# All products but the scores in two halves of 64 columns; the experts' rows turned by VectorE, fetched by blocks of channels

## The chip, the core and the metric

The kernel runs on one core of a Trainium2 chip. A core has TensorE (PE; its weight loads are listed apart as PEld), VectorE (DVE), ScalarE (ACT), GpSimd (POOL) and SyncE (SP, which only issues transfers). TensorE multiplies from SBUF into PSUM, which has eight banks here. Transfers between SBUF and the chip's memory run on 16 DMA engines, and are issued by SP, ACT or GpSimd in the order of each queue. The metric is the device time of one execution, in microseconds; the median of the runs shown is compared.

## The reference

One transformer block on x of 8 x 512 tokens and 256 channels, all in f32. After a layernorm, attention (with a low-rank key/value path) and a mixture of experts run beside each other on the same xn, and both are added to x:

```
xn = layernorm(x)
latent = xn @ w_kv_down                       # 256 -> 128
k, v = split(latent @ w_kv_up)                # 16 heads of 64 each
q = xn @ w_q
att = softmax(causal(q k^T / 8));  y = att v
attention = y @ w_out
scores = sigmoid(xn @ gate_w.T + lb_bias);  top 2 of 8 experts per token
for e in range(8):
    y_e = (silu(xn @ eg[e].T) * (xn @ eu[e].T)) @ ed[e].T     # inner width 128
    moe += where(e chosen, y_e * wmean[e], 0)
shared = (silu(xn @ sg.T) * (xn @ su.T)) @ sd.T               # inner width 256
out = x + attention + moe + shared
```

## The kernel before, in words

The work is cut into 64 pairs of heads: 8 batches of 512 tokens times 8 pairs of the 16 heads. A loop over the pairs writes each engine's order by hand; a plan (`put`, `put_half`) says at which place within a pair's step (0 to 2) the other work is dropped in. Engines follow these orders strictly. TensorE, VectorE, ScalarE, SP and later GpSimd are all ordered in this way.

For each pair, `keys`, `queries` and `values` (L569, L578, L559) are products of weights with the transposed activations; `scores` (L606) multiplies q and k of two heads with a contraction of 64, the two heads in the two row halves of the array. VectorE adds the mask and takes a minimum (L613), ScalarE takes the exponential (L620), VectorE turns the result in 32x32 blocks (`transposed`, L633, L640), and sixteen transfers move the blocks to where they are needed (`moved`, pt<-blk, L652, on SP and GpSimd). Two pairs later `weighted` (L695) multiplies with v: its output has 64 rows for each of two heads, so the two heads use the two column halves of the array. `inverse_sums` (L669 to L674) and `spread_sums` (rb<-row, L682) bring the softmax's sums; GpSimd scales (L708). `project` (L720) multiplies by w_out and takes the shared expert's second product into the same bank; `shared_hidden` (L461) is its first part. All of the products other than scores and `weighted` are full 128x128 ones.

In the first part of the loop the layernorm of the coming batches runs beside the attention: statistics on VectorE, `normalise` (L269) on GpSimd (VectorE for the first batch), `turn` (L279) transposes on TensorE, `logits` (L288). Each token's normalised row goes with its own number in column 256 (a row has 272 columns in all) into `xns`. Then a router on VectorE sorts tokens by expert, and GpSimd scatters the rows into `xg_d` in memory (L440), in 39 tiles of 256 slots, each tile of one expert.

From pair 18 on, the 39 expert tiles run beside the attention. `expert_fetch` gathers the tile's weights (L476, GpSimd) and loads its 256 rows in one transfer on SP (xg<-xg_d, L483). `expert_turn` transposes them on TensorE (four transposes into ps_x, L491), ScalarE copies the result to SBUF (xgT, L493), and GpSimd copies the token numbers (to, L495). `expert_hidden` (ps_e, L503) and `expert_down` (ps_ed, L516) are the products, `expert_add` (L527) adds the result's rows to the output in memory by the token numbers. `expert_fetch` is planned four half steps before the tile's half h, `expert_turn` at the start of step h // 2.

At the start SP and ACT load x and the weights (L135 to L161); a contraction over 256 channels is cut into two chunks of 128, chunk c with the channels 128c to 128c + 127 in the partitions.

Of the kernel before, what the change touches and what calls it, by code (L numbers as in the profile page):

```python
# [29 lines left out]
F32 = mybir.dt.float32  # L33
I32 = mybir.dt.int32
# [14 lines left out]
def kernel(  # L49
# [59 lines left out]
    def bank(shape, name):  # L109

        return psum.tile(shape, F32, tag="w", name=name)

    xf = x.rearrange("b t c -> (b t) c")
    outf = out.rearrange("b t c -> (b t) c")

# [15 lines left out]
    def load_x(b, first=0, count=NQ, by=nc.sync):  # L131
        if b not in xins:
            xins[b] = lnp.tile([P, NQ, C], F32, bufs=3, name="xin")
        n = b * NQ + first
        by.dma_start(  # L135
            xins[b][:, ds(first, count), :],
            xf[ds(n * P, count * P), :].rearrange("(n p) c -> p n c", p=P),
        )

    load_x(0, 0, NQ // 2)  # L140
    load_x(0, NQ // 2, NQ // 2, nc.scalar)
    gate_sb = const.tile([P, NCC, E], F32, name="gate_sb")
# [7 lines left out]
    wq_sb = wts.tile([P, NCC, HD], F32, name="wq_sb")  # L150
    nc.sync.dma_start(wq_sb, w_q.rearrange("(c p) m -> p c m", p=P))
# [3 lines left out]
    nc.sync.dma_start(sg_sb, sg_w)  # L155
    su_sb = wts.tile([P, NCC, NS * P], F32, name="su_sb")
    nc.sync.dma_start(su_sb, su_w)
# [298 lines left out]
    def shared_hidden(b, u):  # L456
        pss = []
        for w in (sg_sb, su_sb):
            ps = bank([P, T], "ps_gu")
            for cc in range(NCC):  # L460
                nc.tensor.matmul(  # L461
                    ps, w[:, cc, ts(u, P)], xnTs[b][:, cc, :],
                    start=(cc == 0), stop=(cc == NCC - 1),
                )
            pss.append(ps)
        th = hp.tile([P, T], F32, name="th")
        h = hp.tile([P, T], F32, tag=f"h{u}", name="h")
        swiglu(*pss, th, h)
        shared[b, u] = h

    fetched, turned, hidden = {}, {}, {}

    def expert_fetch(t):

        w = ep.tile([P, WR], F32, bufs=4, name="w")
        nc.gpsimd.indirect_dma_start(  # L476
            out=w[:, :],
            out_offset=None,
            in_=wall_d[:, :],
            in_offset=bass.IndirectOffsetOnAxis(ap=wrow_i[:, t : t + 1], axis=0),  # L480
        )
        xg = ep.tile([P, NU, W], F32, bufs=3, name="xg")
        nc.sync.dma_start(xg, xg_d[ts(t, SLOTS), :].rearrange("(u p) c -> p u c", p=P))  # L483
        fetched[t] = w, xg

    def expert_turn(t):
        xg = fetched[t][1]
        ps = bank([P, NCC, SLOTS], "ps_x")
        for u in range(NU):
            for cc in range(NCC):  # L490
                nc.tensor.transpose(ps[:, cc, ts(u, P)], xg[:, u, ts(cc, P)], ident)  # L491
        xgT = ep.tile([P, NCC, SLOTS], F32, bufs=2, name="xgT")
        nc.scalar.copy(xgT, ps)  # L493
        to = ep.tile([P, NU], I32, bufs=4, name="to")
        nc.gpsimd.tensor_copy(to, xg[:, :, C].bitcast(I32))  # L495
        turned[t] = xgT, to

    def expert_hidden(t):
        w = fetched[t][0]
        ps = bank([P, 2, SLOTS], "ps_e")  # L500
        for v, at in enumerate((WG, WU)):
            for cc in range(NCC):
                nc.tensor.matmul(  # L503
                    ps[:, v, :], w[:, ds(at + cc * I, I)], turned[t][0][:, cc, :],
                    start=(cc == 0), stop=(cc == NCC - 1),
                )
        th = ep.tile([P, SLOTS], F32, name="the")
        h = ep.tile([P, SLOTS], F32, name="he")
        swiglu(ps[:, 0, :], ps[:, 1, :], th, h)
        hidden[t] = h  # L510

    def expert_down(t):
        w = fetched[t][0]
        ps = bank([P, NU, C], "ps_ed")
        for u in range(NU):
            nc.tensor.matmul(  # L516
                ps[:, u, :], hidden[t][:, ts(u, P)], w[:, ds(WD, C)], start=True, stop=True
            )
# [6 lines left out]
    def expert_add(t, u):  # L525

        nc.gpsimd.indirect_dma_start(  # L527
            out=acc_d[:, :],
            out_offset=bass.IndirectOffsetOnAxis(ap=turned[t][1][:, u : u + 1], axis=0),
            in_=results[t][:, u, :],  # L530
            in_offset=None,
            compute_op=ALU.add,
        )
# [9 lines left out]
    def latent(b):  # L543
        ps = bank([P, T], "ps_lat")
        for cc in range(NCC):
            nc.tensor.matmul(  # L546
                ps, wkd_sb[:, cc, :], xnTs[b][:, cc, :],
                start=(cc == 0), stop=(cc == NCC - 1),
            )
        lats[b] = qkp.tile([P, T], F32, name="lat")  # L550
        nc.scalar.copy(lats[b], ps)  # L551

    def values(b, g, half):

        if half == 0:
            vs[b, g] = vp.tile([P, NQ, VH * D], F32, name="v")
        ps = bank([P, 2, VH * D], "ps_v")
        for u in range(2):
            nc.tensor.matmul(  # L559
                ps[:, u, :],  # L560
                lats[b][:, ts(2 * half + u, P)],
                wkv_sb[:, ds(HD + g * VH * D, VH * D)],
                start=True, stop=True,
            )
        nc.scalar.copy(vs[b, g][:, ts(half, 2), :], ps)

    def keys(b, p):
        ps = bank([P, T], "ps_k")
        nc.tensor.matmul(ps, wkv_sb[:, ts(p, P)], lats[b], start=True, stop=True)  # L569
        ks[b, p] = qkp.tile([P, T], F32, name="k")  # L570
        nc.scalar.copy(ks[b, p], ps)

    def queries(b, p):


        ps = bank([P, T], "ps_q")
        for cc in range(NCC):
            nc.tensor.matmul(  # L578
                ps, wq_sb[:, cc, ts(p, P)], xnTs[b][:, cc, :],
                start=(cc == 0), stop=(cc == NCC - 1),  # L580
            )
        qs[b, p] = qkp.tile([P, T], F32, name="q")
        nc.scalar.mul(qs[b, p], ps, QSCALE)
# [127 lines left out]
    def project(b, tt, ps=None, first=0, last=NS + NPAIR):  # L711


        n = b * NQ + tt
        if ps is None:
            ps = bank([P, C], "ps_o")
        ops = [(yTs.get((b, p)), wo_sb[:, p, :]) for p in range(NPAIR)]
        ops[NPAIR - 2 : NPAIR - 2] = [(shared[b, u], sd_sb[:, u, :]) for u in range(NS)]
        for k, (l, r) in list(enumerate(ops))[first:last]:
            nc.tensor.matmul(  # L720
                ps, l[:, ts(tt, P)], r, start=(k == 0), stop=(k == len(ops) - 1)
            )
# [280 lines left out]
```

## Time and profile before

| | us |
|---|---|
| three runs: median | 955.46 |
| lowest, highest | 953.57, 957.12 |
| the profiled execution, its own time | 949.33 |
| its span on the core | 947.5 |
| granted TensorE clock, mean | 0.987 |

The page lists groups of instructions by line, engine and operation: how many, their busy time and the mean of one, then the idle time of the engine just before them and what ended it. A line "X <- Y" among the waits says that X waited until Y was done: total time, times, and the longest. The chain of work that ended last gives 76% to TensorE, 9% to transfers and 4% to VectorE:

```profile
PE 76%; DMA 9%; DVE 4%; POOL 3%; SPq 3%; issue 2%; ACT 1%; ACTq 0%; DVEq 0%; POOLq 0%
```

Busy time of TensorE counts modelled ends, which overlap the next start, so times of its groups are best read from the starts.

### The profile page before, as it was taken

To read this page: it belongs to the slowest core of one execution; us is meant where nothing else is said; L and a number is where in the kernel's file an instruction comes from. 1 tells how busy PE (TensorE), PEld (TensorE's weight loads), DVE (VectorE), ACT (ScalarE), POOL (GpSimd) and SP (SyncE) were. 2 spreads that over 40 slices of the span, in tenths; PEclk is the share of its full clock that TensorE was granted. 3 is DMA by queue.
4 is the path that set the end of the run, shared out by engine and by line. 5 is a ranking of instruction groups with operands and counts; after the bars stand their busy time and mean duration, and the time that the engine had idled before them with its cause. 6 is when DMAs were issued, how large, how long until landed. Compare 5 with 4: busy or idle time off the path is not lost.

```text
span 947.5 us, 16101 instructions
## 1 busy us (share of the span) xinstructions
PE 912.2 (96%) x4316; PEld 557.6 (59%) x4316; DVE 580.0 (61%) x2041; ACT 504.3 (53%) x1467; POOL 610.2 (64%) x846
## 2 busy tenths in 40 slices
PE   8899898989999979999999999999999999999998
PEld 4355456644455446766667656676666775656656
DVE  3877753897636756356774466743677446675571
ACT  3656553445535546446674366744567545665550
POOL 3698984537887954646766667664767646765560
PEclk9899999999999999999999999999999999999999
DMA  7589888776767789667887777876878868776793
GB/s 274 162 254 283 272 265 296 200 215 207 222 186 187 234 218 220 143 168 183 214 200 171 189 179 176 225 169 160 192 185 207 205 146 196 190 154 147 186 275 96
DMA packets 127449, 190.63 MB, mean 201 GB/s; under 512 B 24896, under 2 KB 88640, under 8 KB 127120
## 3 DMA queue, kind: packets, MB, share of 16 engines
q1 hardware_dynamic: 87728, 103.54, 39.3%
q0 software_dynamic: 37152, 82.52, 36.1%
q10 hardware_dynamic: 2480, 3.55, 1.4%
q8 instruction: 36, 0.59, 0.3%
q14 instruction: 53, 0.43, 0.2%
HBM read 66.45 MB, written 50.18 MB: 123 GB/s over the span
## 4 chain that ended last, share of the span: by engine, by line
PE 76%; DMA 9%; DVE 4%; POOL 3%; SPq 3%; issue 2%; ACT 1%; ACTq 0%; DVEq 0%; POOLq 0%
PE ps_o L720 13%; PE ps_y L695 13%; PE ps_s L606 12%; PE ps_q L578 9%; PE ps_e L503 7%; DMA pt<-blk 5%; PE ps_v L559 4%; PE ps_k L569 4%; PE ps_gu L461 4%; PE ps_ed L516 4%; SPq L652 3%; PE ps_x L491 2%; DMA rb<-row 2%; DVE blk L633 1%; PE ps_lat L546 1%
## 5 line engine op out<-in xcount | busy, mean ns | idle before, releaser
L613 DVE CUSTOM_DVE_ANT_0 ps_s<-ps_s,mask 128x128 f32<-128x128 f32 (+3 forms) x512 | 238.7, 519 | 177.8 <-PE ps_s L606 174.6
L620 ACT ACTIVATE pr<-ps_s,mn 128x128 f32<-128x128 f32 (+3 forms) x512 | 271.1, 538 | 143.6 <-DVE mn L613 113.8
L633 DVE STREAM_TRANSPOSE blk<-pr 128x384 f32<-128x384 f32 (+2 forms) x512 | 207.4, 446 | 26.3 <-ACT yT L707 6.9
L652 POOL DMA_DIRECT2D pt<-blk x303 | 161.5, 654 | 50.6 <-DVE ri L669 21.3
L527 POOL DMA_INDIRECT acc_d<-ye,to x78 | 127.4, 1634 | 91.3 <-issue 29.2
L606 PE MATMUL ps_s<-k,q 64*128 64x128 f32 (+3 forms) x1024 | 167.0, 448 | 6.7 <-ACT pr L620 6.0
L695 PE MATMUL ps_y<-pt,v 128*64 128x512 f32 (+3 forms) x1024 | 153.4, 442 | 10.0 <-DMA pt<-blk 6.3
L708 POOL TENSOR_TENSOR yT<-yT,rb 128x512 f32<-128x512 f32 x62 | 83.0, 1338 | 90.1 <-ACT yT L707 79.1
L606 PEld LDWEIGHTS ps_s<-k,q 64*128 64x128 f32 x1024 | 91.0, 186 | 79.0 <-issue 46.2
L578 PE MATMUL ps_q<-xnT,wq_sb 128*128 128x512 f32 x256 | 124.8, 611 | 0.0
L695 PEld LDWEIGHTS ps_y<-pt,v 128*64 128x64 f32 x1024 | 69.3, 137 | 91.9 <-issue 64.3
L720 PE MATMUL ps_o<-wo_sb,yT 128*128 128x256 f32 x512 | 120.5, 380 | 2.0 <-POOL yT L708 2.0
L620 ACT ACTIVATION_READ_ACCUMULATOR pr<-ps_s,mn 128x1 f32 x512 | 108.7, 212 | 0.0
L720 PEld LDWEIGHTS ps_o<-wo_sb,yT 128*128 128x128 f32 x512 | 96.7, 190 | 17.9 <-POOL yT L708 2.4
L578 PEld LDWEIGHTS ps_q<-xnT,wq_sb 128*128 128x128 f32 x256 | 50.6, 198 | 58.0 <-issue 52.5
L503 PE MATMUL ps_e<-xgT,w 128*128 128x256 f32 x312 | 75.0, 383 | 2.4 <-ACT xgT L493 2.4
L569 PE MATMUL ps_k<-lat,wkv_sb 128*128 128x512 f32 x128 | 71.4, 641 | 1.0 <-ACT lat L551 1.0
L613 DVE DVE_READ_ACCUMULATOR2_ANT mn<- 128x1 f32 x512 | 72.2, 141 | 0.0
L440 POOL DMA_INDIRECT xg_d<-xn,at_i x64 | 62.8, 981 | 14.3 <-issue 12.9
L503 PEld LDWEIGHTS ps_e<-xgT,w 128*128 128x128 f32 x312 | 58.3, 190 | 21.9 <-ACT xgT L493 13.7
L559 PE MATMUL ps_v<-wkv_sb,lat 128*128 128x256 f32 x256 | 67.4, 386 | 0.0
L559 PEld LDWEIGHTS ps_v<-wkv_sb,lat 128*128 128x128 f32 x256 | 46.8, 190 | 31.3 <-issue 18.6
(132 smaller groups left out, 974.9 us busy)
## 6 DMA issues: line engine op xcount, KB each, us to landing
pt<-blk SPq DMA_DIRECT2D x681, 80.0 KB
pt<-blk POOLq DMA_DIRECT2D x303, 80.0 KB
rb<-row SPq DMA_DIRECT2D x128, 128.0 KB
xg_d<-zero POOLq DMA_DIRECT2D x26, 408.0 KB
xg<-xg_d SPq DMA_DIRECT2D x39, 272.0 KB
acc_d<-in_x_dram POOLq DMA_DIRECT2D x8, 512.0 KB
xin<-in_x_dram SPq DMA_DIRECT2D x7, 512.0 KB
xnT_d<-lnT SPq DMA_DIRECT2D x7, 512.0 KB
```

Of the source, the lines that this page charges most:

```text
L503: nc.tensor.matmul(ps[:, v, :], w[:, ds(at + cc * I, I)], turned[t][0][:, cc, :], start=(cc == 0), stop=(cc == NCC - 1),)
L527: nc.gpsimd.indirect_dma_start(out=acc_d[:, :], out_offset=bass.IndirectOffsetOnAxis(ap=turned[t][1][:, u : u + 1], axis=0), in_=results[t ...
L559: nc.tensor.matmul(ps[:, u, :], lats[b][:, ts(2 * half + u, P)], wkv_sb[:, ds(HD + g * VH * D, VH * D)], start=True, stop=True,)
L569: nc.tensor.matmul(ps, wkv_sb[:, ts(p, P)], lats[b], start=True, stop=True)
L578: nc.tensor.matmul(ps, wq_sb[:, cc, ts(p, P)], xnTs[b][:, cc, :], start=(cc == 0), stop=(cc == NCC - 1),)
L606: nc.tensor.matmul(pss[j][:, ds(at, n)], q[ts(j, D), ts(i, P)], k[ts(j, D), :n], start=True, stop=True,)
L613: nc.vector.tensor_tensor_reduce(out=pss[j][:, ds(at, n)], in0=pss[j][:, ds(at, n)], in1=mask[:, T - n :], scale=1.0, scalar=NO_MIN, op0=A ...
L620: nc.scalar.activation(o, s, AF.Exp, bias=mn, scale=-1.0, accum_out=rs[:, j, i : i + 1])
L633: nc.vector.transpose(blk[:, :, j, i : i + (nr - 1) * (NQ - 1) + 1 : NQ - 1, :].rearrange("p b c q -> p c b q"), pr[:, j, : nr * P].rearra ...
L652: by.dma_start(pt[ts(kb, QB), a], blks[b, p][ts(a, QB), kb])
L695: nc.tensor.matmul(ps[ts(j, D), :, c:, :], vs[b, h // VH][:, c, ts(h % VH, D)], pts[b, p][:, :, j, at : at + NQ - c, :], start=(c == 0), s ...
L720: nc.tensor.matmul(ps, l[:, ts(tt, P)], r, start=(k == 0), stop=(k == len(ops) - 1))
```

## The change

1. A helper `product` replaces the full matmul in `latent`, `keys`, `queries`, `values`, `project`, `shared_hidden`, `expert_hidden` and `expert_down`: it makes each product as two matmuls with 64 columns of the weights each, into partitions 0 to 63 and 64 to 127 of the same bank, with the same moving operand. `scores`, `weighted`, `turn`, `logits` and the router's sums stay as they are.
2. `expert_turn` is one VectorE transpose in 32x32 blocks, from SBUF to SBUF, and stands near the end of the step before (place 0.8 of step h // 2 - 1) instead of at the start of step h // 2. TensorE's transposes, ScalarE's copy and GpSimd's copy of token numbers go.
3. For that, `expert_fetch` loads xg with 32 slots in the partitions, in four transfers on SP, one for each block of 64 columns of the row, in pieces of 64 elements. The token numbers of three tiles come in one transfer on ACT.
4. The channels of a row are stored in another order: `normalise` writes runs of 32 channels (`by_chunk`), and wkd, wq, gate, sg and su are loaded in four transfers each (`load_weights`), 32 partitions apiece, with their channels in that order. wq is loaded by ACT, right after its half of x; the gate's weights and bias come later, on SP. The experts' own weights and the remaining loads are unchanged.

```diff
+    def product(out, lhsT, rhs, start, stop):
+        for j in range(2):
+            nc.tensor.matmul(
+                out[ts(j, D)], lhsT[:, ts(j, D)], rhs, start=start, stop=stop
+            )
+    def by_chunk(a):
+        return a.rearrange("p (a c k) -> p c a k", a=NB, k=QB)
...
+    def load_weights(w_sb, w, by=nc.sync):
+        for a in range(NB // NCC):
+            for c in range(NCC):
+                by.dma_start(
+                    w_sb[ds((a * NCC + c) * QB, QB)],
+                    w.rearrange("(x a k) c m -> a c k x m", x=NCC, k=QB)[a, c],
+                )
...
-    gate_sb = const.tile([P, NCC, E], F32, name="gate_sb")
-    nc.scalar.dma_start(gate_sb, gate_w)
-    lb_sb = const.tile([P, E], F32, name="lb_sb")
-    nc.scalar.dma_start(lb_sb, lb_bias.broadcast_to([P, E]))
     wkd_sb = wts.tile([P, NCC, R], F32, name="wkd_sb")
-    nc.sync.dma_start(wkd_sb, w_kv_down.rearrange("(c p) r -> p c r", p=P))
+    load_weights(wkd_sb, w_kv_down.rearrange("(c p) r -> p c r", p=P))
+    wq_sb = wts.tile([P, NCC, HD], F32, name="wq_sb")
+    load_weights(wq_sb, w_q.rearrange("(c p) m -> p c m", p=P), nc.scalar)
...
             by.tensor_scalar(
-                xns[:, n, :C], xins[n // NQ][:, n % NQ, :], mv[:, n, 0:1], rstd[:, n : n + 1],
-                ALU.subtract, ALU.mult,
+                by_chunk(xns[:, n, :C]),
+                xins[n // NQ][:, n % NQ, :].rearrange("p (c a k) -> p c a k", a=NB, k=QB),
+                mv[:, n, 0:1], rstd[:, n : n + 1], ALU.subtract, ALU.mult,
             )
...
-        xg = ep.tile([P, NU, W], F32, bufs=3, name="xg")
-        nc.sync.dma_start(xg, xg_d[ts(t, SLOTS), :].rearrange("(u p) c -> p u c", p=P))
+        xg = ep.tile([P, SLOTS // QB, NCC * QB], F32, bufs=3, name="xg")
+        for a in range(NB):
+            nc.sync.dma_start(
+                xg[ts(a, QB)],
+                xg_d[ts(t, SLOTS), ts(a, NCC * QB)].rearrange("(t q) c -> q t c", q=QB),
+            )
+        if t % NZ == 0:
+            to = ep.tile([P, NZ * NU], I32, bufs=3, name="to")
+            nc.scalar.dma_start(
+                to,
+                xg_d[ts(t // NZ, NZ * SLOTS), C : C + 1]
+                .bitcast(I32).rearrange("(n p) c -> p (n c)", p=P),
+            )
...
     def expert_turn(t):
-        xg = fetched[t][1]
-        ps = bank([P, NCC, SLOTS], "ps_x")
-        for u in range(NU):
-            for cc in range(NCC):
-                nc.tensor.transpose(ps[:, cc, ts(u, P)], xg[:, u, ts(cc, P)], ident)
         xgT = ep.tile([P, NCC, SLOTS], F32, bufs=2, name="xgT")
-        nc.scalar.copy(xgT, ps)
-        to = ep.tile([P, NU], I32, bufs=4, name="to")
-        nc.gpsimd.tensor_copy(to, xg[:, :, C].bitcast(I32))
-        turned[t] = xgT, to
+        nc.vector.transpose(
+            xgT.rearrange("p c (t q) -> p t c q", q=QB),
+            fetched[t][1].rearrange("p t (c k) -> p t c k", k=QB),
+        )
+        turned[t] = xgT
...
-                nc.tensor.matmul(
-                    ps[:, v, :], w[:, ds(at + cc * I, I)], turned[t][0][:, cc, :],
+                product(
+                    ps[:, v, :], w[:, ds(at + cc * I, I)], turned[t][:, cc, :],
                     start=(cc == 0), stop=(cc == NCC - 1),
                 )
...
-        put(h // 2, 0.1, expert_turn, t)
+        put(h // 2 - 1, 0.8, expert_turn, t)
```

More of the change, by code (lines that the diff above doesn't have):

```diff
@@ L138, in load_x @@
         )
+    def load_weights(w_sb, w, by=nc.sync):
[5 more added lines that the diff above has]
+                )
     load_x(0, 0, NQ // 2)
     load_x(0, NQ // 2, NQ // 2, nc.scalar)
-    gate_sb = const.tile([P, NCC, E], F32, name="gate_sb")
-    nc.scalar.dma_start(gate_sb, gate_w)
-    lb_sb = const.tile([P, E], F32, name="lb_sb")
-    nc.scalar.dma_start(lb_sb, lb_bias.broadcast_to([P, E]))
     wkd_sb = wts.tile([P, NCC, R], F32, name="wkd_sb")
-    nc.sync.dma_start(wkd_sb, w_kv_down.rearrange("(c p) r -> p c r", p=P))
+    load_weights(wkd_sb, w_kv_down.rearrange("(c p) r -> p c r", p=P))
+    wq_sb = wts.tile([P, NCC, HD], F32, name="wq_sb")
+    load_weights(wq_sb, w_q.rearrange("(c p) m -> p c m", p=P), nc.scalar)
     wkv_sb = wts.tile([P, 2 * HD], F32, name="wkv_sb")
     nc.sync.dma_start(wkv_sb[:, :HD], w_kv_up[:, :HD])
-    wq_sb = wts.tile([P, NCC, HD], F32, name="wq_sb")
-    nc.sync.dma_start(wq_sb, w_q.rearrange("(c p) m -> p c m", p=P))
+    gate_sb = const.tile([P, NCC, E], F32, name="gate_sb")
+    load_weights(gate_sb, gate_w)
+    lb_sb = const.tile([P, E], F32, name="lb_sb")
+    nc.sync.dma_start(lb_sb, lb_bias.broadcast_to([P, E]))
     nc.sync.dma_start(wkv_sb[:, HD:], w_kv_up[:, HD:])
@@ L154 @@
     sg_sb = wts.tile([P, NCC, NS * P], F32, name="sg_sb")
-    nc.sync.dma_start(sg_sb, sg_w)
+    load_weights(sg_sb, sg_w)
     su_sb = wts.tile([P, NCC, NS * P], F32, name="su_sb")
-    nc.sync.dma_start(su_sb, su_w)
+    load_weights(su_sb, su_w)
     sd_sb = wts.tile([P, NS, C], F32, name="sd_sb")
@@ L469, in shared_hidden @@
         shared[b, u] = h
-    fetched, turned, hidden = {}, {}, {}
+    fetched, tokens, turned, hidden = {}, {}, {}, {}
     def expert_fetch(t):
@@ L481, in expert_fetch @@
         )
-        xg = ep.tile([P, NU, W], F32, bufs=3, name="xg")
-        nc.sync.dma_start(xg, xg_d[ts(t, SLOTS), :].rearrange("(u p) c -> p u c", p=P))
+        xg = ep.tile([P, SLOTS // QB, NCC * QB], F32, bufs=3, name="xg")
[11 more added lines that the diff above has]
+            )
+            for u in range(NZ):
+                tokens[t + u] = to[:, ts(u, NU)]
         fetched[t] = w, xg
     def expert_turn(t):
-        xg = fetched[t][1]
-        ps = bank([P, NCC, SLOTS], "ps_x")
-        for u in range(NU):
-            for cc in range(NCC):
-                nc.tensor.transpose(ps[:, cc, ts(u, P)], xg[:, u, ts(cc, P)], ident)
-        xgT = ep.tile([P, NCC, SLOTS], F32, bufs=2, name="xgT")
-        nc.scalar.copy(xgT, ps)
-        to = ep.tile([P, NU], I32, bufs=4, name="to")
-        nc.gpsimd.tensor_copy(to, xg[:, :, C].bitcast(I32))
-        turned[t] = xgT, to
+        xgT = ep.tile([P, NCC, SLOTS], F32, bufs=2, name="xgT")
+        nc.vector.transpose(
[3 more added lines that the diff above has]
+        turned[t] = xgT
     def expert_hidden(t):
@@ L502, in expert_hidden @@
             for cc in range(NCC):
-                nc.tensor.matmul(
-                    ps[:, v, :], w[:, ds(at + cc * I, I)], turned[t][0][:, cc, :],
+                product(
+                    ps[:, v, :], w[:, ds(at + cc * I, I)], turned[t][:, cc, :],
                     start=(cc == 0), stop=(cc == NCC - 1),
@@ L515, in expert_down @@
         for u in range(NU):
-            nc.tensor.matmul(
+            product(
                 ps[:, u, :], hidden[t][:, ts(u, P)], w[:, ds(WD, C)], start=True, stop=True
@@ L528, in expert_add @@
             out=acc_d[:, :],
-            out_offset=bass.IndirectOffsetOnAxis(ap=turned[t][1][:, u : u + 1], axis=0),
+            out_offset=bass.IndirectOffsetOnAxis(ap=tokens[t][:, u : u + 1], axis=0),
             in_=results[t][:, u, :],
@@ L545, in latent @@
         for cc in range(NCC):
-            nc.tensor.matmul(
+            product(
                 ps, wkd_sb[:, cc, :], xnTs[b][:, cc, :],
@@ L558, in values @@
         for u in range(2):
-            nc.tensor.matmul(
+            product(
                 ps[:, u, :],
@@ L568, in keys @@
         ps = bank([P, T], "ps_k")
-        nc.tensor.matmul(ps, wkv_sb[:, ts(p, P)], lats[b], start=True, stop=True)
+        product(ps, wkv_sb[:, ts(p, P)], lats[b], start=True, stop=True)
         ks[b, p] = qkp.tile([P, T], F32, name="k")
@@ L577, in queries @@
         for cc in range(NCC):
-            nc.tensor.matmul(
+            product(
                 ps, wq_sb[:, cc, ts(p, P)], xnTs[b][:, cc, :],
@@ L719, in project @@
         for k, (l, r) in list(enumerate(ops))[first:last]:
-            nc.tensor.matmul(
+            product(
                 ps, l[:, ts(tt, P)], r, start=(k == 0), stop=(k == len(ops) - 1)
```

## The prediction

> **What bounds the kernel now.** I read the stretches first, because the share of one engine over the whole span hides where it is full.
>
> ```profile
> PE 912.2 (96%) x4316; PEld 557.6 (59%) x4316; DVE 580.0 (61%) x2041; ACT 504.3 (53%) x1467; POOL 610.2 (64%) x846
> ```
> ```profile
> core 0: us, PE busy (x) PEld busy (x) DVE busy (x) ACT busy (x) POOL busy (x), PEclk, DMA share, GB/s
> 0.00:247.00 247.00, 227.80 (x1036) 122.86 (x1038) 171.01 (x626) 129.63 (x380) 165.62 (x256) 0.97 0.79 243
> 247.00:345.00 98.00, 88.16 (x396) 48.59 (x394) 58.58 (x213) 47.83 (x147) 78.14 (x132) 0.97 0.72 209
> 345.00:860.00 515.00, 512.61 (x2486) 331.76 (x2483) 306.88 (x1054) 293.67 (x837) 329.10 (x400) 1.00 0.79 184
> 860.00:947.50 87.50, 83.62 (x404) 54.41 (x402) 43.57 (x150) 33.17 (x104) 37.39 (x60) 1.00 0.66 175
> ```
>
> The third stretch, in which all 39 expert tiles run, has TensorE idle for 2.4 of 515 us, with every other engine at 57 to 64%. What TensorE is spared there comes off the time, microsecond for microsecond. Before 345 us TensorE idles 29 us, waiting for transfers and GpSimd; there a saving can be swallowed.
>
> Then the timeline of TensorE in that stretch. Its columns are start, length, line, tile, shape; the difference of two starts is what a group really takes, since the ends are modelled.
>
> ```profile
> 407.04 1.03 PE L720 MATMUL ps_o<-wo_sb,yT 128*128 128x256 f32 x4
> 408.00 2.43 PE L606 MATMUL ps_s<-k,q 64*128 64x512 f32 x16
> 410.36 2.38 PE L695 MATMUL ps_y<-pt,v 128*64 128x512 f32 x16
> 412.66 0.66 PE L491 MATMUL ps_x<-ident,xg 128*128 128x128 f32 x4
> 413.15 1.03 PE L516 MATMUL ps_ed<-w,he 128*128 128x256 f32 x4
> 414.02 1.02 PE L569 MATMUL ps_k<-lat,wkv_sb 128*128 128x512 f32 x2
> 414.88 1.88 PE L578 MATMUL ps_q<-xnT,wq_sb 128*128 128x512 f32 x4
> ```
>
> An f32 product is two passes: ps_k takes (414.88 - 414.02)/2 = 0.43 us a pass of 512 columns, ps_ed 0.87/4 = 0.217 a pass of 256. So four ps_o passes are 0.86, but 0.96 pass before the scores begin: 0.10 us of draining, at a change of the array's division (128*128 to 64*128). Over the trace the gaps at all 245 such changes have this 92 to 97 ns in the median.
>
> **Part 1, products in two halves of 64 columns.** The trace already has this form: ps_y, two heads in two halves. One head has 2 x (512 + 384 + 256 + 128) = 2560 columns, 2.15 us at 0.43 per 512; both took 412.66 - 410.36 = 2.30, with 0.10 of it the drain. So the halves run beside each other and two halves cost what one full product does. Within it, starts of like passes are 430 ns apart at 512 columns and 216 at 256: no loss.
>
> [...] The loads of ps_y in the same stretch:
>
> ```profile
> 411.27 0.14 PEld L695 LDWEIGHTS ps_y<-pt,v 128*64 128x64 f32 x2 [0.28 <-issue]
> 411.59 0.14 PEld L695 LDWEIGHTS ps_y<-pt,v 128*64 128x64 f32 x2 [0.18 <-issue]
> ```
>
> Two loads fit in 0.14 us and begin while TensorE streams without a gap. Only the first pass after a change of division shows its load: 480 ns instead of 430 (+50) in halves, 533 instead of 427 (+106) with 128 columns, +57 for a transpose. [...]
>
> What it removes is changes. I counted them in the order of TensorE's instructions: 245 before, 203 after (products and ps_y now share a division; scores, the layernorm's transposes and logits remain). At 96 ns plus the exposed load of the new division, that is 43.6 us before and 35.2 after: **-8.4 us** (up to pair 17 +0.6, pairs 18 to 61 -7.9, then -1.1).
>
> What it adds is instructions: 8632 loads and matmuls become 12136, and at 256 columns four must arrive every 216 ns, 54 ns each. At 343.6 us, after a wait of 5.5 us with an empty queue, six of ps_y's instructions start within 0.1 us, and the queue meets the semaphore wait of the ps_x behind its 32 instructions 0.1 us after the first load. So issue is far faster than 54 ns; cost 0, upper end in the rivals. 43 more waits of TensorE on itself look at least ten matmuls back: 0.
>
> **Part 2, no transposes on TensorE.** ps_x takes 0.109 a transpose (0.49 for four with 0.057 for the first load): 39 x 4 x 0.109 = **-17.0 us**, all in the full stretch. TensorE's waits for the copy behind them (ps_e on ACT xgT) total 2.4 us: **-2.4**. In return:
>
> ```profile
> L633 DVE STREAM_TRANSPOSE blk<-pr 128x384 f32<-128x384 f32 x256 | 136.1, 547 | 22.4 <-ACT yT L707 6.9 <-ACT pr L620 5.3 <-DMA pt<-blk 3.5
> L633 DVE STREAM_TRANSPOSE blk<-pr 128x256 f32<-128x256 f32 x128 | 47.6, 409 | 0.2 <-ACT pr L620 0.2
> L493 ACT COPY xgT<-ps_x 128x512 f32<-128x512 f32 x39 | 22.9, 588 | 0.0
> L483 SPq DMA_DIRECT2D xg<-xg_d x39: 363/538/1000, 339.6 to 820.1; - x39
> L682 SPq DMA_DIRECT2D rb<-row x128: 609/629/1941, 38.4 to 929.3; - x128
> SPq L652 <- DVE blk L633: 129.0, 30, 11.4
> ```
>
> A 128x512 transpose: 547 + (547 - 409) = 0.69 us, x39 = 27 us on VectorE, which has 208 us idle in the stretch. It stands at the end of a step, behind riT; queued behind it are the next pair's mask-and-minimum (L613), which waited 89 us for scores in the 34 steps, 2.6 each. That idle hides it; without it TensorE would wait 0.69 a tile, 27 us. The turn now waits for xg on VectorE. In the sampled step SP begins xg at 424.93; four transfers at 0.67 instead of one at 0.6 put the last one's issue at 427.6 and its landing near 430, while VectorE is due at the turn about 432 and must be at scores at 438.6. Cost 0; 1 us a tile (39) if it is late past both.
>
> SP gets 39 x 3 more transfers: 117 x 0.67 = 78 us. In 345 to 860 it waited 129 us for blocks and 36 for rows; that covers it, leaving some 60 with the shorter stretch. Behind it are pt<-blk, needed two pairs later. ACT gets 13 token transfers at 0.6 to 0.8 (8 to 10 us), loses 22.9 of copies: no cost. The first waits for the scatters while TensorE there idles for pt anyway. GpSimd loses 39 copies of 0.27.
>
> [...] xg now has 1024 pieces of 256 B (before 256 of 1088 B at 61 ns mean, 0.98 us over 16 engines). The trace's packets take 27 ns at 512 B and 11 at 64 B in the median: about 18 at 256, 1.15 us a tile. [...] I take 18 ns; no SBUF write that small from DRAM is in the trace.
>
> **Part 3, loads by blocks and the permuted layernorm.** Up to the first blk SP has 13 more transfers of 0.5 us, 6.5, against its wait of 15.9 there. ACT issues four pieces of wq with waits for landings (xin 4.3, first piece, wkd 5.1), so its table load ends near 8 us; its first copy is due at 8.98. wq landed at 11.84 and q began at 11.93: between -1 and +3 us, taken as 0. normalise writes in runs of 32: GpSimd's nearest row with such runs, yT, takes 1338 ns for 512 elements against 1216 for normalise's 256, so runs are not what costs; 0, up to +10 us if it doubled (28 rows, and ps_t already waits 17 us for it).
>
> **Sum.** -8.4 - 17.0 - 2.4 = -27.8; I give 2 us back for the tail, where pt and the last output set the pace. 947.5 - 26 = 921.5 span, 923.3 with the 1.8 around it (949.33). The runs' median of 955.46 is 6.1 above that execution, so **929.5 us** for the median.
>
> **Rivals.** *Half given back (12%).* SP or VectorE becomes late at the turn by 0.35 us a tile: 39 x 0.35 = 14, 943 us. For: SP loses over half its slack. Against: 6 us between turn and scores. *Nothing gained (5%).* As much is lost again at xg as TensorE gains, 955. *Issue decides (7%, slower).* TensorE's queue is fed at over 54 ns an instruction in the runs of 256-column halves (ps_o up to 160 in a row). From 58 to 59 ns the whole gain is gone, as 682 products x 2 passes x 4 instructions pay; at 62 ns 1364 x 32 ns = 44, 973 us. For: no stretch of the trace holds 54 ns over more than 64 instructions. Against: 343.6 us. *Loads exposed (4%).* [...] All else, 72%, is the forecast, with its own range 923 to 937.
>
> **Numbers.** Half a per cent, 4.8 us, is about what a measurement of this kernel can tell from no change. Faster 0.83 (forecast, nearly all of the half gain), same 0.06, slower 0.11. The range 922 to 953 leaves out the slower cases and little below.
>
> **What will show it.** ps_x gone; ps_ed and ps_e halves 216 ns apart at 256 columns, else issue or load rivals are right; TensorE idle still under 10 us in the expert stretch, now some 25 us shorter; turns of 0.69 us, with VectorE's wait before them for xg under 0.3 each; SP's wait for blk down to about half. A VectorE that waits for xg and scores that come late for it, or packets of 256 B at 50 ns, would make the forecast wrong.

## The result, and the profile after

The changed kernel takes 964.46 us in the median of 20 runs (955.84 to 973.1); the kernel before, run beside it, 957.21 (950.26 to 963.65, 20 runs). The ratio is **1.0064**, with a 95% interval of 1.0041 to 1.0087. Instead of 26 us less it is some 6 us more, outside the predicted range. The ratios here and below are formed from fast executions alone, so they can differ a little from the quotient of two medians.

The profiled execution spans 963.4 us at a mean granted clock of 0.973. First come the busy line of its page, then the four stretches that were shown of before (same columns; the last one ends later):

```profile
PE 903.1 (94%) x6068; PEld 470.3 (49%) x6068; DVE 602.4 (63%) x2080; ACT 482.0 (50%) x1428; POOL 606.8 (63%) x807
```
```profile
0.00:247.00 247.00, 224.92 (x1304) 105.73 (x1306) 163.13 (x597) 124.26 (x361) 158.30 (x243) 0.95 0.79 234
247.00:345.00 98.00, 89.94 (x526) 41.43 (x522) 51.07 (x184) 44.18 (x136) 76.52 (x129) 0.95 0.70 196
345.00:860.00 515.00, 491.63 (x3527) 265.34 (x3529) 334.12 (x1114) 270.69 (x800) 318.58 (x358) 0.98 0.81 184
860.00:963.40 103.40, 96.63 (x716) 57.78 (x712) 54.06 (x186) 42.87 (x134) 53.43 (x78) 1.00 0.68 178
```

In the third stretch TensorE idled 2.4 us before; now it idles 23, and its clock, 1.00 before, is 0.98. It does have less to do: here are the same instructions as in the sample of before, from TensorE's timeline of the same pair (columns as there; each product now counts twice as many instructions).

```profile
424.46 1.03 PE L117 MATMUL ps_o<-wo_sb,yT 128*64 128x256 f32 x8
425.42 2.43 PE L640 MATMUL ps_s<-k,q 64*128 64x512 f32 x16
427.78 2.37 PE L729 MATMUL ps_y<-pt,v 128*64 128x512 f32 x16
429.98 1.03 PE L117 MATMUL ps_ed<-w,he 128*64 128x256 f32 x8
430.85 1.03 PE L117 MATMUL ps_k<-lat,wkv_sb 128*64 128x512 f32 x4
431.70 1.89 PE L117 MATMUL ps_q<-xnT,wq_sb 128*64 128x512 f32 x8
```

From the start of ps_s to that of ps_q it took 6.88 us before (408.00 to 414.88) and takes 6.28 now. The four transposes of ps_x are gone, and ps_y runs into ps_ed without a change of division. The halves cost what the prediction said: ps_ed's four pairs of passes take 0.87 us to the next start, as four whole ones did. So TensorE's side of the sum is there to see, and the time is lost in waits. Three views show where. First the waits of VectorE, from 345 to 880 us (total, times, longest); the third line is that of before:

```profile
DVE xgT L526 <- DMA xg<-xg_d: 47.9, 11, 8.6
DVE ps_s L647 <- PE ps_s L640: 45.4, 15, 9.5
DVE ps_s L613 <- PE ps_s L606: 98.3, 29, 10.2
```

The turn waits for its rows, 48 us that did not exist, and the wait for scores that was to hide it has halved from 98.3. Then SP's waits in the same stretch, with one line of before at the end:

```profile
SPq L508 <- DMA to<-xg_d: 19.0, 4, 8.5
SPq L716 <- DMA row<-riT: 14.3, 5, 5.1
SPq L686 <- DMA to<-xg_d: 13.9, 3, 6.1
SPq L716 <- DMA to<-xg_d: 13.5, 3, 6.8
SPq L686 <- DVE blk L667: 9.4, 6, 2.4
SPq L652 <- DVE blk L633: 135.4, 31, 11.4
```

SP waits 46 us for `to`, a transfer that ACT issues; its spare time, read from what it waits for blocks, is down from 135 us to 9. And the start of the kernel, from the timeline (an idle time in brackets, with what ended it):

```profile
1.33 8.91 ACTq L157 DMA_DIRECT2D wq_sb<-in_w_q_dram  x4
...
10.27 1.28 ACT L305 ACT_TABLE_LOAD   x1 [10.27 <-DMA gate_sb<-in_gate_w_dram]
11.56 1.07 ACT L305 COPY xnT<-ps_t 128x512 f32<-128x512 f32 x2
12.68 3.40 PE L117 MATMUL ps_lat<-xnT,wkd_sb 128*64 128x512 f32 x8 [2.84 <-ACT xnT L305]
...
18.51 2.31 PE L117 MATMUL ps_q<-xnT,wq_sb 128*64 128x512 f32 x6 [2.43 <-issue]
```

The four pieces of wq keep ACT until 10.2 us; the first copy comes at 11.56 (8.98 before), the first queries at 18.51 (11.93 before).

In the long stretch SP's waits for `to` and VectorE's waits for xg are one cause. A bad place in the timeline of all engines shows how:

```profile
489.86 0.71 DVE L526 STREAM_TRANSPOSE xgT<-xg 128x512 f32<-128x512 f32 x1
490.00 2.43 PE L640 MATMUL ps_s<-k,q 64*128 64x512 f32 x16
...
490.11 0.39 ACTq L514 DMA_DIRECT2D to<-xg_d  x1
494.05 1.79 SPq L508 DMA_DIRECT2D xg<-xg_d  x4
...
498.29 0.71 DVE L526 STREAM_TRANSPOSE xgT<-xg 128x512 f32<-128x512 f32 x1 [7.73 <-DMA xg<-xg_d]
498.93 0.67 DVE L647 CUSTOM_DVE_ANT_0 ps_s<-ps_s,mask 128x512 f32<-128x512 f32 x1
...
499.74 0.69 ACT L654 ACTIVATE pr<-ps_s,mn 128x512 f32<-128x512 f32 x1 [8.95 <-DVE mn L647]
...
500.57 1.95 PE L117 MATMUL ps_e<-xgT,w 128*64 128x256 f32 x16 [2.21 <-ACT pr L654]
```

ACT issues `to` at 490.11, behind its other work. In this trace landings are recorded under semaphores, numbers that later instructions wait for. The 1078 transfers of SP and ACT share eight of them (100 to 106 and 108; GpSimd's have 110 to 117). All but the first of each number wait for their own number before they are issued, and in the 1.5 us after such an issue no landing is recorded under it: by these records the transfer that had the number before has landed by then. `to` has number 104, and its last part lands at 494.04; SP's next rows have 104 too, and start at 494.05. After twelve of the thirteen transfers of `to` SP's next one with the same number starts within 0.12 us of the landing. VectorE reaches that tile's turn at 490.6 and stands there until 498.3. Behind it in its queue are the minima of scores that TensorE had begun at 490.00; behind these ACT's exponentials stand 8.95 us; behind these TensorE waits at ps_y and ps_e.

### The profile page after: what moved, and what is told of

Same layout as the page of the kernel before. It is cut to its first block, busy times and chain, and to the rows that moved or that the text cites. A ratio compares the mean times of both kernels' runs of the same rounds, so it can differ in the third digit from the quotient of the medians.

```text
span 963.4 us, 19725 instructions
## 1 busy us (share of the span) xinstructions
PE 903.1 (94%) x6068; PEld 470.3 (49%) x6068; DVE 602.4 (63%) x2080; ACT 482.0 (50%) x1428; POOL 606.8 (63%) x807
## 4 chain that ended last, share of the span: by engine, by line
PE 66%; DMA 11%; issue 6%; POOL 5%; DVE 5%; SPq 5%; ACT 1%; ACTq 0%; POOLq 0%; DVEq 0%
PE ps_o L117 14%; PE ps_y L729 11%; PE ps_s L640 10%; PE ps_q L117 8%; PE ps_e L117 5%; PE ps_k L117 4%; PE ps_gu L117 4%; PE ps_v L117 4%; DMA pt<-blk 4%; SPq L686 4%; PE ps_ed L117 2%; DMA xg<-xg_d 2%; DVE ps_s L647 2%; DMA acc_d<-ye,to 2%; PE ps_lg L311 2%
## 5 line engine op out<-in xcount | busy, mean ns | idle before, releaser
L117 PE MATMUL ps_q<-xnT,wq_sb 128*64 128x512 f32 x512 | 127.8, 619 | 2.8 <-issue 2.8
L729 PEld LDWEIGHTS ps_y<-pt,v 128*64 128x64 f32 x1024 | 74.5, 140 | 104.5 <-issue 78.1
L117 PE MATMUL ps_o<-wo_sb,yT 128*64 128x256 f32 x1024 | 121.0, 379 | 1.2 <-issue 1.2
L117 PEld LDWEIGHTS ps_o<-wo_sb,yT 128*64 128x64 f32 x1024 | 76.8, 137 | 36.4 <-issue 3.4
L117 PE MATMUL ps_k<-lat,wkv_sb 128*64 128x512 f32 x256 | 74.2, 648 | 2.3 <-ACT lat L585 1.0
L117 PEld LDWEIGHTS ps_q<-xnT,wq_sb 128*64 128x64 f32 x512 | 39.6, 144 | 75.2 <-issue 67.0
L117 PE MATMUL ps_e<-xgT,w 128*64 128x256 f32 x624 | 74.2, 379 | 2.2 <-ACT pr L654 2.2
L463 POOL DMA_INDIRECT xg_d<-xn,at_i x64 | 63.0, 984 | 14.3 <-issue 14.1
L117 PE MATMUL ps_v<-wkv_sb,lat 128*64 128x256 f32 x512 | 67.9, 383 | 0.0
L708 POOL DMA_DIRECT2D row<-riT x64 | 49.3, 771 | 20.0 <-DVE riT L706 9.8
L117 PEld LDWEIGHTS ps_e<-xgT,w 128*64 128x64 f32 x624 | 45.9, 137 | 31.6 <-issue 9.4
```

Source lines behind the costliest of these rows:

```text
L117: nc.tensor.matmul(out[ts(j, D)], lhsT[:, ts(j, D)], rhs, start=start, stop=stop)
L463: ins = nc.gpsimd.indirect_dma_start(out=xg_d[:, :], out_offset=bass.IndirectOffsetOnAxis(ap=at_i[:, k, n : n + 1], axis=0), in_=xns[:, n, :],
L708: nc.gpsimd.dma_start(row.rearrange("a x q -> (a x) q"), riT)
L729: nc.tensor.matmul(ps[ts(j, D), :, c:, :], vs[b, h // VH][:, c, ts(h % VH, D)], pts[b, p][:, :, j, at : at + NQ - c, :], start=(c == 0), s ...
```

## The experiments

The theory after this reading is that the gain on TensorE is real, and that it is eaten by (a) the start and (b) the turn that waits for xg, with the tokens' transfer as its main cause. The rivals are that the halves cost time themselves, or that SP is late by its own work. All ratios are to the kernel before in the same session (medians 957 to 960), with their 95% intervals.

To see where in the kernel a trace differs, I take the starts of the pairs' scores. The columns are microseconds: the first scores, pairs 0 to 16 (layernorm, router, the first scatters), 16 to 25 (scatters, first expert), 25 to 58 (experts), and from there to the end.

| kernel | first | 0-16 | 16-25 | 25-58 | 58-end |
|---|---|---|---|---|---|
| before | 15.4 | 217.4 | 120.3 | 496.7 | 97.7 |
| before_again | 15.3 | 217.2 | 132.9 | 497.2 | 98.1 |
| changed | 23.7 | 215.1 | 132.9 | 492.5 | 99.2 |
| e1_halves | 15.5 | 213.4 | 135.9 | 499.9 | 97.1 |
| e3_startup | 15.6 | 218.1 | 135.4 | 494.9 | 98.7 |
| e4_tokens | 23.7 | 217.7 | 134.8 | 478.3 | 98.9 |
| e5_late | 23.2 | 215.6 | 132.9 | 548.0 | 97.4 |
| e6_both | 15.4 | 219.4 | 137.0 | 483.4 | 98.1 |
| e7_full | 15.1 | 217.5 | 131.9 | 481.7 | 99.3 |
| e8_early | 15.5 | 219.8 | 130.7 | 480.8 | 97.4 |
| e9_pool | 15.5 | 217.6 | 137.4 | 475.8 | 97.5 |
| e10_pool_full | 15.4 | 214.0 | 132.7 | 477.8 | 99.0 |
| e11_halves_late | 15.4 | 212.0 | 139.8 | 476.2 | 97.4 |
| e12_first_turn | 15.5 | 216.1 | 134.6 | 481.9 | 96.5 |
| e13_halves_14 | 15.2 | 217.2 | 139.5 | 478.7 | 97.3 |

**Before, once more.** No edit; a second profile.

> The kernel before once more, for a second profile. The first one spanned 947.5 us, while the median of the runs lies at 955 to 960. Theory: the difference of some 8 us lies in the pairs before the experts (16 to 24), where a wait of TensorE of over 1 us is followed by some 4 us at about half the clock, and in a second profile the scores of pair 25 begin some 5 to 10 us later than in the first, with the expert pairs 25 to 58 as long as in the first within 1 us. Rival: the runs differ by the same share everywhere.

The span is 960.7. Pairs 25 to 58 take 497.2 us against 496.7, pairs 16 to 25 take 12.6 us more, as expected. In these nine pairs TensorE idles 20.2 us instead of 9.8, and has half its clock for 20.5 us instead of 6.8. Not every stop of over 1 us is followed by half the clock there: in the first trace those of 1.49 and 5.50 us (ending at 252.9 and 343.6) come with 3.41 us of it each, the one of 2.03 us (ending at 264.8) with none. So the profiled execution that the prediction was worked on was a lucky one in the scatters' pairs. In the column 16-25 two traces of one kernel differ by over 10 us. In "25-58" these two differ by 0.5, but e9_pool, e11_halves_late and e13_halves_14, whose programs are the same in those pairs, read 475.8 to 478.7, and e12_first_turn, which differs only in one turn before them, 481.9. So differences of up to 6 us there, and of over 10 in the columns before, count only where repeated times show them.

**Halves alone** (before, with `product` in place of all matmuls but scores, ps_y and the transposes).

> The kernel before with its products in two halves of 64 columns, and nothing else changed. The transposes ps_x stay on TensorE, and so there are 271 changes of the array's division, where before had 245 and the changed kernel has 203; at 96 ns and the exposed load of the new division that is 47.7 us against 45.9, so by the theory (halves cost what full products do) it stands at 0 to +2 us against before, 0.999 to 1.003. Rival one, the halves themselves cost what was lost (issue, or loads that show): +15 us or more, and ps_ed's passes of 256 columns more than 216 ns apart.

964.47 us, 1.0067 (1.0047 to 1.0086): 6 us slower. That is more than the theory's 0 to 2, and under the rival's 15. The passes keep their 216 ns, so issue and loads are not what costs. Among the experts the trace loses 2.7 us to the second profile of before; the count had said 1.8 over the kernel. Where the rest lies this trace does not show: up to pair 25 it is no longer than the second one of before.

**The start** (changed kernel).

```diff
-    load_weights(wq_sb, w_q.rearrange("(c p) m -> p c m", p=P), nc.scalar)
+    load_weights(wq_sb, w_q.rearrange("(c p) m -> p c m", p=P))
```

> The changed kernel with the four pieces of wq on SP's queue, straight behind wkd's, so that ACT's queue holds only half of x ahead of its table load. Theory: the first scores were 8.3 us late because the last piece of wq landed at 18.4 us and the table load ended at 11.5; here the first copy of xnT is back near 9 us and wq lands by 13, the first scores start within 2 us of before's, and the time is 6 to 8 us below the changed kernel's, about 957. Rival: the late start is taken up by slack before the experts, and the time stays at 964 within 2 us.

960.6 us, 0.9998 (0.9968 to 1.0028), against 1.0064: 0.66%, 6 us, the low end of what the theory had. Its timeline:

```profile
1.31 1.28 ACT L305 ACT_TABLE_LOAD   x1 [1.31 <-PEq L1021]
3.20 2.84 SPq L157 DMA_DIRECT2D wq_sb<-in_w_q_dram  x4
8.44 0.59 ACT L305 COPY xnT<-ps_t 128x512 f32<-128x512 f32 x1 [5.85 <-PE ps_t L302]
...
12.14 1.89 PE L117 MATMUL ps_q<-xnT,wq_sb 128*64 128x512 f32 x8
```

The same four pieces issue in 2.84 us instead of 8.91. It was their place in the queues, not their number.

**The tokens** (changed kernel).

```diff
-            nc.scalar.dma_start(
+            nc.gpsimd.dma_start(
                 to,
```

> The changed kernel with the 13 transfers of tokens issued by GpSimd instead of ACT. Theory: SP's 46 us of waits for these transfers are gone, xg lands earlier, VectorE's wait at the turn falls from 48 us to about 25, and the time falls by 5 to 10 us, to 955 to 960. Rival: SP is late by its own work, four transfers for xg instead of one; then its waits move to other names, VectorE's wait at the turn stays above 40 us, and the time stays within 2 us of 964.

954.35 us, 0.9926 (0.99 to 0.9952), against 1.0064: 1.4%, 13 us, more than expected. Pairs 25 to 58 take 478.3 us instead of 492.5. Waits of SP and then of VectorE, 345 to 880 us:

```profile
SPq L686 <- DVE blk L667: 38.8, 14, 6.3
SPq L716 <- DMA row<-riT: 36.7, 14, 6.2
```
```profile
DVE xgT L526 <- DMA xg<-xg_d: 16.9, 4, 10.0
```

None of `to` is left among SP's waits, and it waits again for what others make, 75 us, so it has time to spare. The turn's wait falls from 47.9 us to 24 (these 16.9, and 7.1 that stand under pt). Thirteen small transfers on ACT's queue had cost this. The rival, SP late by its own four transfers, falls. The edit also takes the thirteen issues of 0.37 us off ACT, 5 us in all on an engine that is busy half of the time; this share was not separated.

**The turn later** (changed kernel).

```diff
-        put(h // 2 - 1, 0.8, expert_turn, t)
+        put(h // 2, 0.1, expert_turn, t)
```

> The changed kernel with the turn of the experts' rows one third of a pair later, at the place where before had its transposes on TensorE: behind the minima of the next pair's scores on VectorE and not ahead of them. Theory: VectorE's wait for xg falls from 48 us to under 15, nothing that TensorE needs is queued behind it any longer, and the time falls by 10 to 15 us, to 950 to 955. Rival one: the turn now stands just before the product that reads it, and ps_e waits for it, 1 us or more a tile, so that the gain is under 5 us. Rival two: xg comes late whatever the place, and TensorE waits for it at ps_e as long as it does now: no change.

1016.6 us, 1.0603 (1.0552 to 1.0653). The theory's remedy was wrong. It is rival one, and far worse than that said. The wait for xg at the turn is gone, and TensorE's largest wait is now this one:

```profile
PE ps_e L117 <- ACT pr L654: 28.9, 12, 2.6
```

A place in the timeline shows the chain:

```profile
702.21 0.58 DVE L667 STREAM_TRANSPOSE blk<-pr 128x384 f32<-128x384 f32 x1 [0.24 <-issue]
...
703.55 0.73 DVE L667 STREAM_TRANSPOSE blk<-pr 128x256 f32<-128x256 f32 x2
...
704.21 0.67 DVE L526 STREAM_TRANSPOSE xgT<-xg 128x512 f32<-128x512 f32 x1
...
704.98 1.30 PE L117 MATMUL ps_e<-xgT,w 128*64 128x256 f32 x10 [2.57 <-issue]
```

The turn stands behind eight minima and the first transposes of blocks, so it ends at 704.9, while TensorE was ready at 702.4. Such stops bring a second cost: from 345 us on TensorE has half its clock for 48 us in this trace, for 17 in the changed kernel's, and for 2 and 7 in the two of before. So of the two places that of the change is by far the better one; what was wrong is that xg came late to it.

**Both repairs** (e3_startup and e4_tokens together).

> The changed kernel with wq's pieces on SP and the tokens' transfers on GpSimd, both. The two alone were worth 0.66% and 1.4% of the time. Theory: they are two separate causes, one before the first scores and one among the experts, and add up to 16 us or more below the changed kernel, about 943 to 949. Rival: what the earlier start brings is taken up again before the experts (its trace alone ended only 0.8 us earlier), and the time is that of the tokens alone, 954.

949.24 us, 0.9879 (0.9847 to 0.9912). Within the intervals the two add up (0.66 and 1.38 points alone, 1.85 together). The kernel is now faster than before by 1.2%.

**Whole products** (e6_both, `product` as one matmul of 128 columns).

> The kernel of e6_both with each product whole again, 128 columns at once, so that of the change only the turn on VectorE and the transfers in pieces are left. TensorE then has 245 changes of division instead of 203, 45.9 instead of 35.9 us. Theory: where TensorE is the bound the halves are worth what these changes cost, less the 4 us that the halves lost beyond the count when they stood alone; this kernel is 4 to 8 us slower than e6_both. Rival: the halves bring nothing, or lose, as they did alone (6 us); then this kernel is equal to e6_both or up to 6 us faster.

945.09 us, 0.986 (0.9821 to 0.9898): as fast as with halves, so it is the rival. But pair by pair the trace disagrees with a plain "halves bring nothing": in pairs without a wait e6_both is 0.20 us shorter than e7_full, every time (14.3 and 14.1, 12.6 and 12.4, 10.9 and 10.7), which makes 6.6 us over these 33 pairs; single waits elsewhere hide it in the sum.

**Rows earlier** (e6_both; the fetch of xg split from that of the weights).

```diff
+        put_half(h - 4 if t < NZ else h - 5, 0.5, rows_fetch, t)
         put_half(h - 4, 0.5, expert_fetch, t)
```

> The kernel of e6_both with the rows of each expert tile but the first three fetched half a pair earlier, in a fourth buffer. Theory: what VectorE still waits at the turn (24 us with the tokens on GpSimd) falls under 8 us, and the time is 5 to 8 us below e6_both. Rival: what is left of the wait is of the first tiles, behind the last scatters, or hidden behind TensorE's own work, and the time is that of e6_both within 2 us.

948.9 us, 0.9893 (0.9858 to 0.9929). The wait at the turn falls from 22.8 us to 7.3 (e6_both's line, then this one's) and the time stays, so it is the rival: what was left of that wait was mostly hidden.

```profile
DVE xgT L526 <- DMA xg<-xg_d: 22.8, 5, 9.4
DVE xgT L529 <- DMA xg<-xg_d: 7.3, 1, 7.3
```

**Less on GpSimd** (e8_early).

```diff
-                moved(*pairs[m], 8 if m >= END else 5)
+                moved(*pairs[m], 8 if m >= END else 3)
```

> The kernel of e8_early with three instead of five of each pair's sixteen block transfers (pt) on GpSimd in the pairs with experts, and two more on SP. In e8_early TensorE's waits among the experts (10 us) are for weights, spread sums and blocks whose transfers GpSimd issued late. Theory: GpSimd has become the pace in the short steps; freed of 2 x 0.6 us a pair it keeps up, and the time falls by 4 to 8 us, to 941 to 945. Rival: GpSimd is late because it waits for its own sums in memory (acc_d), not because of what it issues, or SP becomes late in its place; then the time stays within 2 us of 949 or rises.

947.67 us, 0.987 (0.9837 to 0.9902). Pairs 25 to 58 are 5 us shorter in the trace, which is within what chance does there, and the time is inside the interval of e8_early's. It is the rival.

**Whole products, and halves late** (e9_pool with whole products; then with halves from pair 22).

```diff
+        if not in_halves:
+            nc.tensor.matmul(out, lhsT, rhs, start=start, stop=stop)
+            return
...
+        in_halves = m >= E0
```

> The kernel of e9_pool with each product whole again. In the pairs without a wait the halves gave 0.20 us a pair (6.8 us from pair 25 to 58), and e6_both and e7_full were equal all the same. Theory: the gain was given back in waits for GpSimd; with those gone this kernel is 4 to 8 us slower than e9_pool. Rival: the halves lose as much before the experts as they gain among them, whatever GpSimd does; then this kernel is within 2 us of e9_pool.

> The kernel of e9_pool with whole products up to pair 21 and halves from pair 22 on, where the experts begin. Theory of e10 (halves cost nothing before the experts): equal to e9_pool within 2 us. Its rival (they lose some 5 us there): 3 to 6 us faster than e9_pool, and pair 25 begins some 5 us earlier than with halves throughout.

e10_pool_full takes 944.91 us, 0.9868 (0.9819 to 0.9917), the same as e9_pool, so GpSimd's work is not what levels halves and whole products. e11_halves_late takes **939.46** us, 0.9771 (0.9733 to 0.981). By the ratios that is a full per cent, 9 us, faster than either, and by the medians 5 and 8 us. So what the halves give among the experts agrees with what the prediction had counted there, 7.9 us, and they lose about as much before them.

**In which pairs they lose** (e11_halves_late, with `m >= S0`, pair 14).

> The kernel of e11_halves_late with halves from pair 14 on instead of pair 22, that is in the pairs of the scatters too; whole products only in the layernorm's and router's pairs. If the halves lose in the scatters' pairs (where TensorE waits for ACT and transfers), this is as slow as e9_pool, 947; if they lose in the pairs of the layernorm, whose transposes and logits have another division than halves, it is as fast as e11_halves_late, 939.

944.41 us, 0.985 (0.9804 to 0.9897): like e9_pool, and 0.8% (7.6 us) slower than e11_halves_late; against e12_first_turn below, which was run beside it and has halves from pair 22 too, it is 6 us, with intervals that just overlap. By these times it is the pairs of the scatters, where TensorE stops for transfers and for ACT, not those of the layernorm with their changes of division. The single traces do not show it: from pair 14 to 22 they take 121 and 122 us with halves (e9_pool and this one) and 124 and 123 without (e11_halves_late and e12_first_turn).

**The first tile's turn** (e11_halves_late, the turn of tile 0 alone at place 0.3 of its own pair).

> The kernel of e11_halves_late with the turn of the first expert tile alone put behind the minima of the pair that uses it (that product comes at two thirds of its pair, so it doesn't wait as it did in e5_late). In e11_halves_late VectorE stands 9.5 us at this turn until the last scatters and the rows' transfer have landed; TensorE idles 8.0 us behind it and then has half its clock for one product (4.54 us instead of 2.37). Theory: most of these 10 us goes, less what the pair then waits for blocks, as before did there (5.5 us): 3 to 8 us below e11_halves_late, 931 to 936. Rival: the blocks of that pair, which SP moves behind the same transfer, are as late; no change within 2 us.

940.21 us, 0.9787 (0.9741 to 0.9833): no change, as the rival said. In e11_halves_late's timeline and then in this one's:

```profile
352.93 2.23 SPq L516 DMA_DIRECT2D xg<-xg_d  x4
...
357.34 4.54 PE L737 MATMUL ps_y<-pt,v 128*64 128x512 f32 x16 [8.02 <-DMA xg<-xg_d]
...
357.95 0.71 DVE L534 STREAM_TRANSPOSE xgT<-xg 128x512 f32<-128x512 f32 x1 [9.48 <-DMA xg<-xg_d]
```
```profile
353.12 2.52 SPq L516 DMA_DIRECT2D xg<-xg_d  x4
355.76 1.30 SPq L724 DMA_DIRECT2D rb<-row  x2
...
357.11 3.25 PE L737 MATMUL ps_y<-pt,v 128*64 128x512 f32 x8 [7.01 <-DMA xg<-xg_d]
```

VectorE no longer waits at the turn, and TensorE's stop stays, 7.0 us for 8.0: SP itself stands at the first xg until the scatters have landed, with the sums (rb) of the pair behind it.

## Why the prediction was wrong

**What held.** Two halves cost what a whole product does: 216 and 430 ns a pass, and runs of over 160 loads and matmuls keep that pace, 54 ns each. Both slower rivals fall with that: within such runs neither issue nor weight loads add to the 216 and 430 ns, and no run shows loads exposed there. The count of changes held among the experts: 0.20 us a pair, 6.6 us from pair 25 to 58; e11_halves_late against e10_pool_full, 9 us by the ratios, each of which is known to about 5. The turn instead of ps_x held as well: with whole products and both repairs (e7_full) pairs 25 to 58 take 481.7 us instead of 497, 15 of the 19 us said, with 9 us of waits still in it. A turn takes 0.71 us; a 256 B packet 18 ns in the median, as estimated, with a DMA share of 0.81 in the expert stretch (0.79 before). The normalise in runs cost nothing (1217 ns each on GpSimd, before 1216).

**The step that failed first: "The turn now waits for xg on VectorE ... Cost 0".** It rested on SP beginning xg where it did in before's trace, and on "ACT gets 13 token transfers at 0.6 to 0.8 ...: no cost". That priced the transfers on the queue that issues them. They cost SP, whose next transfer waited for the one of ACT on the same semaphore, 46 us in all, and through xg and VectorE they cost 13 us of time (e4_tokens). The turn's wait for xg was put at 0 and is 48 us over 39 tiles, and the cover that was to hide it, VectorE's wait for scores, shrank from 98 us to 45. A VectorE that waits for xg is one of the signs that the prediction itself had named against its forecast. Its rival "half given back" had the place of the loss, a turn late by 0.35 us a tile, 14 us, though not its cause: it was nearly the right price, held for unlikely. SP's spare time itself was judged well: with the tokens elsewhere 75 us are left, for "some 60".

**The second: Part 3, "between -1 and +3 us, taken as 0".** The first scores came 8.3 us late, 6 us of the time. The step saw that ACT would wait for landings and put the end of its table load near 8 us; it ended at 11.55. ACT waited three times for the transfer that had the same semaphore before: for half of x, for half of wkv and for a piece of gate_sb, which SP had issued late for the same reason. The last piece of wq, which the step judged only by the old single transfer (11.84), landed at 18.4.

**The third: "up to pair 17 +0.6".** With halves in the scatters' pairs the kernel is, by the ratios, 7.6 us (e13_halves_14) to 9.5 us (e9_pool) slower than without, each to about 6. The step counted changes of division in a stretch where TensorE is not the bound; it had itself said that there "a saving can be swallowed", but not that something can be lost. Why it is lost stays open. A part may be the clock: over the runs the mean granted clock is 0.979 in these two and 0.983 in e11_halves_late, which is about 40 us at half the clock against 32, an estimate of 4 us of the 8. But it is 0.980 in e10_pool_full and 0.981 in e12_first_turn, which do not have halves there, so this is not shown, and what would make TensorE stop there more often, or longer, was not found.

**The sum closes.** e11_halves_late is 2.3% below before. Adding halves in the early pairs (+1.0), the start (+0.7) and the tokens (+1.4) gives +0.8%; measured is +0.64, with each term known to about 0.4. This says once more, as e6_both did, that the terms add up, and is no separate test of them. So a kernel with nearly the predicted gain exists: 939.5 us, 20.7 below its before, where 26 had been said. It also has the rows fetched earlier and fewer transfers on GpSimd, two edits that moved the time by no more than its noise (e8_early, e9_pool).

## What to carry to other kernels

A moved or added transfer has to be priced on every queue that shares its semaphores, not only on the one that issues it (here 13 transfers on ACT made SP wait 46 us): ask which transfer has to land before the next issue, and how late the issuing engine comes to it. Where an engine that works in order gets a new wait, its cover has to be read from what is queued behind it, and the remedy that paid here was to make the data early (e4_tokens, 1.4% faster than the changed kernel), not to put the work late (e5_late, 52 us slower). And a change that pays where an engine is the bound can be switched on only there: with halves from pair 22 on, the same edit was worth about 1% instead of nothing.

## What was not expected of the hardware

**The clock falls in steps.** In the traces of before and of the changed kernel the granted clock is 1.0 or 0.5, and the stretches at 0.5 that end within the trace are 3.41 or 6.83 us long. Here are windows of e9_pool (columns as above) with one that adds up to 6.8, and TensorE's timeline there:

```profile
136.00:140.00 4.00, 1.00 (x8) 0.40 (x8) 0.00 (x0) 0.00 (x0) 4.00 (x5) 0.91 0.62 207
140.00:144.00 4.00, 3.50 (x12) 1.44 (x14) 1.81 (x6) 2.21 (x6) 3.92 (x8) 0.50 0.92 263
144.00:148.00 4.00, 4.00 (x24) 2.16 (x22) 1.74 (x7) 1.93 (x7) 3.18 (x4) 0.74 0.96 253
```
```profile
140.50 4.54 PE L732 MATMUL ps_y<-pt,v 128*64 128x512 f32 x16 [3.50 <-DMA rb<-row]
```

After a stop of 3.5 us ps_y takes 4.54 us instead of 2.37, so that the stop costs 5.7 us at least. In before's trace a stop of 1.49 us that ended at 252.9 was followed by 3.41 us at half the clock, while in e10_pool_full one of 1.79 that ended at 152.2 was followed by none. What decides between them is not shown. The two traces of before show what this does to single executions: 6.8 and 20.5 us at half the clock in pairs 16 to 25, beside 10 us more of stops.

**Small transfers on another queue.** Thirteen transfers of tokens, 0.37 us each to issue on ACT, cost 13 us of the kernel (e4_tokens), and the trace shows them at work through the semaphores that ACT's queue shares with SP's.
